# Weight folds and the attention of an expert layer, packed on row groups of TensorE

## The chip, the cores and the metric

The kernel runs on one core of a Trainium2 chip. A core has five engines that run side by side and wait for each other by semaphores: TensorE (PE in the profile; PEld is its weight load), VectorE (DVE), ScalarE (ACT), GpSimd (POOL) and SyncE (SP), which here issues nearly all DMAs. The metric is the device time of one execution in microseconds; the kernel before took 2024.21 us, the median of 3 runs (2023.55 to 2026.4).

## The reference

Sixteen sequences of 64 tokens with 128 features pass through two layers. Each layer has a cross attention to 1601 context rows, a state-space scan, and a feed-forward part. Layer 0's feed-forward part is a mixture of eight experts that begins with a small attention of its own. Two pieces matter here. The cross attention (16 heads of 64):

```python
q = ln @ Wq
kv = kv_input @ Wkv
logits = einsum('bhld,bhsd->bhls', q * scale, k * scale)
out = einsum('bhls,bhsd->bhld', softmax(logits), v)
return out @ Wo
```

and the small attention at the head of the experts (4 heads of 32; keys and values have one head that the four share):

```python
nx = _rmsnorm(X, g1)
Q = (nx @ Wq.T).reshape(B, S, 4, 32).transpose(0, 2, 1, 3)
Kc, Vc = nx @ Wkc.T, nx @ Wvc.T
attn = softmax(einsum('bhsd,btd->bhst', Q, Kc) * scale)
out = einsum('bhst,btd->bhsd', attn, Vc)
X = X + out.transpose(0, 2, 1, 3).reshape(B, S, d) @ Wo.T
```

All numbers are float32.

## The kernel before

**The main loop.** The cross attention is a chain of 64 groups (2 layers, 16 sequences, 2 halves of 8 heads), each with 13 tiles of 128 context rows. `step` does one tile of one group: a scores product `s` of 512 columns (line 651), its copy to `st` by ScalarE and a running maximum `R` by VectorE, and, 21 steps behind, four products `av` of 129 columns (line 713) that average the context with the softmaxed weights. In between lie the maximum's transposes (`tm`), its spread over the partitions (`mb`), the subtraction and the exponential (lines 700 and 701). 832 such steps make the span.

**Folds.** The weights are folded ahead: `fold` multiplies, for each head, the 64 rows of `WqT` with those of `WkT` into `wqk`, and those of `WvT` with `Wo` into `wvo`. Each of the two folds of each of the two layers has 4 groups of 4 heads, so there are 16 groups with 4 products of 128x128 over 64 rows. `raw_pair` (line 317) loads one group's weights with partitions 0 to 63 holding the rows of one head and the four heads side by side in the free dimension. The four results fill one PSUM tile, and one instruction scales and evicts them: ScalarE in two groups of the first fold, VectorE elsewhere.

**The expert layer.** `moe` (line 904) is called for four stages of 256 tokens (`CG` = 2 blocks of 128, `BG` = 4 sequences). After a norm and a transpose to `xT` its small attention goes: queries `mq`, two heads per PSUM tile, each head on partitions 0 to 31 (line 929); keys `mk` on 32 partitions; values `mv`, one sequence after the other on 64 partitions; scores `ms`, 8 products over 32 rows whose 128 outputs are two heads of one sequence; the softmax on VectorE and ScalarE; transposes `mt` to 64 partitions with a copy `pt` each; the averages `ma`, 8 products over 64 rows (line 979); and the output `mo`, for each of the two blocks four accumulated products over 32 rows, one per head (line 988). The router and the experts follow.

**What sets the order.** `run` walks through the steps and puts other work between them: `prep` holds the folds, queries and contexts by their step, and `between` holds the scans, expert layers and feed-forwards, which advance by a budget of estimated VectorE time. Each `yield` with a number charges that budget, and `yield HOP` lets two steps pass. `behind` ties such work behind the instructions of the step before it; apart from that a scheduler orders each engine's instructions when the program is built. Each engine then works through its queue in order, and so does SP's queue of DMA issues.

**PSUM.** Three pools: `pss` with three tiles for scores, `psa` for the averages, and `pst` with three tiles in rotation. `tp` (line 93) hands out the latter to everything else: folds, transposes, expert layers. A fourth request has to wait until the first tile has been evicted.

**Shape of the profile's names.** A float32 product is two records in the trace, with a weight load each; a transpose is one.

Of the kernel before, what the change touches and what calls it, by code (L numbers as in the profile page):

```python
# [32 lines left out]
F32 = mybir.dt.float32  # L33
# [3 lines left out]
AF = mybir.ActivationFunctionType  # L37
ALU = mybir.AluOpType
AX = mybir.AxisListType
# [3 lines left out]
P = 128  # L43
NB, L, D = 16, 64, 128
# [6 lines left out]
H, DH = 16, 64  # L51
# [22 lines left out]
CG = 2  # L74
TG = CG * P
BG = 2 * CG
# [3 lines left out]
class Kernel:  # L80
# [130 lines left out]
    def setup(self):  # L211
# [24 lines left out]

        self.xed = [self.dram.tile([NB, D + 1], F32, tag=f"xed{lay}", name=f"xed{lay}") for lay in range(2)]
        latents, fold, queries, context = self.latents(0, 0), self.fold_qk(0), self.queries(0, 0), self.first_context()
        next(latents)

# [5 lines left out]
        for g in (latents, context, fold, latents, fold, context, queries, queries, context, queries):  # L246
            next(g)
        nc.vector.tensor_scalar_mul(self.nvcol, self.vcol, -1.0)
        self.in_order()
        return (0, context), (1, fold), (5, queries), (8, latents)  # L250

    def setup_rest(self):
# [64 lines left out]
    def raw_pair(self, lay, l, r, g, queue):  # L317


        if lay == 0:  # L320
            t = self.at.tile([P, 2, NQ], F32, tag="st2", name=f"raw{l}{g}", bufs=11)
            pair = [t[:DH, i, :].rearrange("p (h d) -> p h d", h=4) for i in range(2)]
        else:
            pair = [self.at.tile([DH, 4, D], F32, tag="raw", name=f"raw{n}{g}", bufs=3) for n in (l, r)]
        for t, n in zip(pair, (l, r)):
            queue.dma_start(out=t, in_=self.a[f"L{lay}{n}"].rearrange("(h j) d -> j h d", j=DH)[:, g * 4:g * 4 + 4, :])
        return pair

    def fold(self, lay, dst, l, r, scale):

        nc = self.nc
        for g in range(H // 4):
            if (lay, l) == (0, "WqT"):
                raw = self.raw0[g]
            else:
                raw = self.raw_pair(lay, l, r, g, nc.sync)
            if lay == 0 and l == "WvT":
                yield HOP3
            t = self.tp(f"{l}{lay}{g}")
            for k in range(4):  # L340
                nc.tensor.matmul(t[:, k * D:(k + 1) * D], raw[0][:, k, :], raw[1][:, k, :], start=True, stop=True)
            to = dst[:, g * 4:g * 4 + 4, :].rearrange("p h d -> p (h d)")
            if (lay, l) == (0, "WqT") and g < 2:
                nc.scalar.activation(to, t, AF.Copy, scale=scale)
            else:
                nc.vector.tensor_scalar_mul(to, t, scale)
            yield 0.7

    def fold_qk(self, lay):
# [554 lines left out]
    def moe(self, gr):  # L904
        nc, tc, a = self.nc, self.tc, self.a
        X = self.X[:, gr * CG:(gr + 1) * CG, :]
        with tc.tile_pool(name="mo1", bufs=1) as one, tc.tile_pool(name="mo2", bufs=2) as work:
            t1 = lambda shape, name: one.tile(shape, F32, tag=name, name="mo_" + name)
            ld = lambda name, shape, src=None: self.load(name, shape, a[name] if src is None else src, one)
            fWqT, fWkvT = ld("fWqT", [P, D]), ld("fWkvT", [P, 64])  # L910
            fWoT = ld("fWoT", [32, 4, D], a["fWoT"].rearrange("(h k) n -> k h n", k=32))
            WrT = ld("WrT", [P, NE])
            xi, nx, xT = t1([P, CG, D], "xi"), t1([P, CG, D], "nx"), t1([P, TG], "xT")
            mv, (r, rr) = self.moments(X, CG, [LN, LNRMS])
# [6 lines left out]
            self.transpose_tokens(xT, nx, CG, f"mot{gr}", G1)  # L921
            yield HOP

            q, kT, v = t1([32, BG, 4, L], "q"), t1([32, TG], "kT"), t1([L, BG, 32], "v")
            for hh in range(2):
                t = self.tp(f"mq{hh}")
                for k in range(2):
                    h = hh * 2 + k
                    nc.tensor.matmul(t[:32, k * TG:(k + 1) * TG], fWqT[:, h * 32:(h + 1) * 32], xT, start=True, stop=True)
                nc.scalar.copy(  # L930
                    q[:, :, hh * 2:hh * 2 + 2, :],
                    t[:32, :].rearrange("p (h b l) -> p b h l", h=2, l=L),
                )
                yield 0.7
            t = self.tp("mk")
            nc.tensor.matmul(t[:32, :TG], fWkvT[:, :32], xT, start=True, stop=True)
            nc.scalar.copy(kT, t[:32, :TG])
            t = self.tp("mv")
            for b in range(BG):
                nc.tensor.matmul(t[:L, b * 32:(b + 1) * 32], xT[:, b * L:(b + 1) * L], fWkvT[:, 32:], start=True, stop=True)  # L940
            nc.scalar.copy(v.rearrange("p b n -> p (b n)"), t[:L, :BG * 32])
            yield 0.3
            yield HOP

            n = 2 * BG
            shape = [P, n, L]
            sc = t1(shape, "sc")
            t = self.tp("ms")
            for i in range(n):
                b, hp = i // 2, i % 2  # L950
                nc.tensor.matmul(t[:, i * L:(i + 1) * L], q[:, b, 2 * hp:2 * hp + 2, :].rearrange("p h l -> p (h l)"), kT[:, b * L:(b + 1) * L], start=True, stop=True)
            t3 = t.rearrange("p (n l) -> p n l", l=L)
            m = self.sm([P, n], "mm")
            nc.vector.tensor_reduce(m, t3, AX.X, ALU.max)
            nc.vector.tensor_tensor(sc, t3, self.bc(m, shape), ALU.subtract)
            nc.scalar.activation(sc, sc, AF.Exp, scale=32.0 ** -0.5)
            yield 1.4
            yield HOP1
            d, r = self.sm([P, n], "md"), self.sm([P, n], "mr")
            nc.vector.tensor_reduce(d, sc, AX.X, ALU.add)  # L960
# [1 line left out]
            nc.vector.tensor_tensor(sc, sc, self.bc(r, shape), ALU.mult)  # L962
            yield 1.5
            yield HOP
            oT = t1([32, 4, TG], "oT")
            pts = []
            for g in range(n // 4):
                t = self.tp(f"mt{g}")
                for i in range(4):
                    nc.tensor.transpose(t[:L, i * P:(i + 1) * P], sc[:, g * 4 + i, :], self.ident)  # L970
                pt = work.tile([L, 512], F32, tag="pt", name=f"mpt{g}")
                nc.vector.tensor_copy(pt, t[:L, :])
                pts.append(pt)
                yield 0.7
            yield HOP
            for g, pt in enumerate(pts):
                o = self.tp(f"ma{g}")
                for i in range(4):
                    nc.tensor.matmul(o[:32, i * P:(i + 1) * P], v[:, g * 2 + i // 2, :], pt[:, i * P:(i + 1) * P], start=True, stop=True)
                for j in range(2):  # L980
                    b = g * 2 + j
                    nc.scalar.copy(oT[:, :, b * L:(b + 1) * L], o[:32, j * 256:(j + 1) * 256].rearrange("p (h l) -> p h l", h=4))
                yield 0.1
            yield HOP
            o = self.tp("mo")
            for k in range(CG):
                for h in range(4):
                    nc.tensor.matmul(o[:, k * D:(k + 1) * D], oT[:, h, k * P:(k + 1) * P], fWoT[:, h, :], start=(h == 0), stop=(h == 3))
            xs = xi.rearrange("p c d -> p (c d)")
            nc.vector.tensor_tensor(xs, xs, o[:, :CG * D], ALU.add)  # L990
            nc.gpsimd.tensor_tensor(X, X, xi, ALU.add)
# [643 lines left out]
```

## Time and profile before

| | |
|---|---|
| median of 3 runs | 2024.21 us |
| the profiled execution | 2023.47 us |
| its span, first to last instruction | 2021.7 us |
| PE busy | 1974.8 us (98%) |
| VectorE busy | 1563.8 us (77%) |
| ScalarE busy | 1382.3 us (68%) |
| GpSimd busy | 520.5 us (26%) |
| scores `s` (line 651), PE busy | 853.0 us |
| averages `av` (line 713), PE busy | 868.1 us |
| folds (line 341), PE busy, all four | 5.5 + 4.6 + 4.6 + 4.6 us |
| `mq`, `mk`, `mv`, `ms`, `mt`, `ma`, `mo` (four stages) | 7.8, 2.4, 2.6, 8.0, 4.3, 7.7, 8.2 us |

A group's line gives the line of the source, the engine, the operation, what is written from what, the rows and columns of the array that the product uses, the shape, the count, the busy time with the mean length of one record, and the idle time of the engine just before, with what ended it. Products overlap in the array, so a record is longer than the distance to the next one, and busy times of neighbouring groups overlap by that. The rows of ten digits cut the span into 40 slices; a digit is the busy share in tenths.

### The profile page before, as it was taken

The page shows a single profiled execution, that of the slowest core. Times are in us where ns is not written, and L with a number is a line of the kernel's source. Part 1 is how long each engine was busy: PE and PEld are TensorE (multiplying, and loading weights), DVE is VectorE, ACT ScalarE, POOL GpSimd, SP SyncE. Part 2 cuts the span into 40 slices and gives each one's busy share as a digit, 9 for nine tenths or more (in the row PEclk, how much of TensorE's full clock was granted, in tenths as well). Part 3 has the DMA queues.
Part 4 walks back from the last instruction along what each step waited for, and adds up shares of the span by engine and source line. Part 5 has one row for each costly group of instructions (what it writes and reads, how often), then busy time and mean ns, then how long its engine had stood idle before and what let it go on. Part 6 is the DMA issues. An engine that isn't in the chain of part 4 may idle for free. (4 is left out here: it accounts for less than half of the span.)

```text
span 2021.7 us, 32901 instructions
## 1 busy us (share of the span) xinstructions
PE 1974.8 (98%) x12123; PEld 1499.8 (74%) x12123; DVE 1563.8 (77%) x2954; ACT 1382.3 (68%) x2628; POOL 520.5 (26%) x579
## 2 busy tenths in 40 slices
PE   9999999999999989999999999999999999999998
PEld 6777777676777767778777787777778777787787
DVE  6977777886778887676988777898686979778884
ACT  5788878887768887566767657776565656666561
POOL 5111123542123442121543203542111121002000
PEclk9999999999999999999999999999999999999999
DMA  6111112321122321221221102221110110101000
GB/s 175 63 59 46 46 42 84 84 73 50 43 66 84 83 70 36 65 76 45 67 80 51 36 24 72 71 62 51 44 53 18 57 36 22 55 18 36 23 1 22
DMA packets 141805, 110.54 MB, mean 55 GB/s; under 512 B 11458, under 2 KB 127950, under 8 KB 141646
## 3 DMA queue, kind: packets, MB, share of 16 engines
q1 hardware_dynamic: 141102, 108.19, 18.5%
q8 instruction: 96, 1.57, 0.3%
q14 instruction: 63, 0.52, 0.1%
q10 hardware_dynamic: 544, 0.26, 0.0%
HBM read 79.97 MB, written 27.41 MB: 53 GB/s over the span
## 5 line engine op out<-in xcount | busy, mean ns | idle before, releaser
L713 PEld LDWEIGHTS av<-kv,st 128*128 128x128 f32 x6656 | 851.6, 192 | 317.3 <-issue 288.7
L713 PE MATMUL av<-kv,st 128*128 128x129 f32 x6656 | 868.1, 276 | 6.5 <-DVE aq L722 3.9
L651 PE MATMUL s<-qT,kvT 128*128 128x512 f32 x1664 | 853.0, 602 | 17.2 <-DVE R L665 14.2
L700 DVE TENSOR_TENSOR st<-st,mb 128x1024 f32<-128x1024 f32 (+1 forms) x448 | 501.7, 1132 | 1.3 <-PE mb L692 1.1
L701 ACT ACTIVATE st<-st 128x1024 f32<-128x1024 f32 (+1 forms) x448 | 444.9, 997 | 72.1 <-DVE st L700 68.8
L656 ACT ACTIVATE st<-s,mcol 128x512 f32<-128x512 f32 x416 | 283.5, 685 | 221.2 <-PE s L651 178.6
L658 ACT COPY st<-s 128x512 f32<-128x512 f32 x416 | 240.3, 581 | 130.4 <-PE s L651 103.1
L651 PEld LDWEIGHTS s<-qT,kvT 128*128 128x128 f32 x1664 | 259.6, 192 | 84.8 <-DVE R L665 36.1
L663 DVE SCALAR_TENSOR_TENSOR R<-s,mcol,R 128x512 f32<-128x512 f32 x352 | 262.0, 744 | 69.8 <-ACT st L656 68.4
L665 DVE TENSOR_TENSOR R<-s,R 128x512 f32<-128x512 f32 x352 | 240.9, 685 | 90.4 <-ACT st L658 89.3
L762 POOL TENSOR_TENSOR aq<-aq,rd 128x512 f32<-128x512 f32 x63 | 77.6, 1232 | 409.9 <-DVE rd L761 402.6
L565 POOL TENSOR_TENSOR kv<-kv,vec 128x384 f32<-128x384 f32 (+1 forms) x128 | 137.6, 1094 | 151.0 <-PE kt L625 71.7
L866 POOL TENSOR_TENSOR db<-sc_u,bb 128x512 f32<-128x512 f32 x64 | 84.7, 1326 | 134.4 <-DVE h L877 60.8
L883 POOL TENSOR_TENSOR sc_y<-sc_y,h 128x512 f32<-128x512 f32 x60 | 79.9, 1332 | 104.2 <-DVE h L882 80.0
L877 DVE TENSOR_TENSOR_SCAN h<-da,db 128x512 f32<-128x512 f32 x64 | 85.3, 1333 | 0.0
L616 ACT ACTIVATE kv<-kv,coff,crstd 128x128 f32<-128x128 f32 x182 | 76.5, 489 | 5.1 <-POOL coff L613 5.1
L665 DVE TENSOR_TENSOR R<-s,st 128x512 f32<-128x512 f32 x32 | 22.1, 689 | 72.3 <-ACT st L658 72.3
L607 ACT ACTIVATE scr<-kv,cmean 128x128 f32<-128x128 f32 x182 | 72.8, 400 | 6.9 <-DVE cmean L603 3.7
L722 DVE SCALAR_TENSOR_TENSOR aq<-xeb,ee,av 128x129 f32<-128x129 f32 x252 | 72.8, 341 | 1.4 <-PE av L713 1.3
L135 POOL TENSOR_TENSOR crstd<-cvar,neghalf 128x13 f32<-128x13 f32 x14 | 35.0, 2502 | 134.6 <-DVE cvar L611 134.4
L450 PE MATMUL q<-xnT,wqk 128*128 128x128 f32 x512 | 68.8, 277 | 0.0
L450 PEld LDWEIGHTS q<-xnT,wqk 128*128 128x128 f32 x512 | 62.9, 192 | 6.3 <-issue 3.1
(410 smaller groups left out, 1973.5 us busy)
## 6 DMA issues: line engine op xcount, KB each, us to landing
bb<-bcd SPq DMA_DIRECT2D x64, 256.0 KB, 4.4
xh<-kv SPq DMA_DIRECT2D x16, 832.0 KB, 4.8
kv<-xh SPq DMA_DIRECT2D x16, 832.0 KB, 5.5
kvT<-xhT SPq DMA_DIRECT2D x16, 800.0 KB, 4.5
xhT<-kvT SPq DMA_DIRECT2D x15, 800.0 KB, 3.4
kv<-in_ctx_dram SPq DMA_DIRECT2D x15, 768.0 KB, 5.5
ew<-in_e1T_dram SPq DMA_DIRECT2D x36, 64.0 KB, 1.9
ew<-in_e3T_dram SPq DMA_DIRECT2D x36, 64.0 KB, 1.9
```

The lines of the kernel that those rows point to most:

```text
L450: nc.tensor.matmul(t[:, k * P:(k + 1) * P], self.wqk[:, g * 4 + k, :], xnT, start=True, stop=True)
L565: nc.gpsimd.tensor_tensor(kv[:, lo:hi, :D], kv[:, lo:hi, :D], self.row(self.vec[:, w1, :], [P, hi - lo, D]), ALU.mult)
L651: mm = nc.tensor.matmul(s, self.kv_of[lay, b][1][:, i * P:(i + 1) * P], q, start=True, stop=True)
L656: ev = nc.scalar.activation(st, s, AF.Identity, bias=mc)
L658: ev = nc.scalar.copy(st, s)
L663: mx = nc.vector.scalar_tensor_tensor(R, s, mc, last, ALU.add, ALU.max)
L665: mx = nc.vector.tensor_tensor(R, s, last, ALU.max)
L700: nc.vector.tensor_tensor(st, st, self.row(mb, [P, n, NQ]), ALU.subtract)
L701: nc.scalar.activation(st, st, AF.Exp)
L713: nc.tensor.matmul(o, st, self.kv_of[lay, b][0][:, i, :], start=(i == 0 and k % 2 == 0), stop=(i == NT - 1 and k % 2 == 1))
L866: nc.gpsimd.tensor_tensor(db, u, self.row(bb[:, 0, s % 2, :], both), ALU.mult)
L877: nc.vector.tensor_tensor_scan(flat(h), flat(da), flat(db), 0.0, ALU.mult, ALU.add)
```

## The change

The folds, and every product of the small attention that used 32 or 64 of the array's 128 rows, are laid out again.

- `raw_pair` loads the weights as they lie, 128 rows of two heads on 128 partitions, and `fold` multiplies the even heads from partitions 0 to 63 and the odd heads from 64 to 127, in turn, into two PSUM tiles. Each tile is evicted by an instruction of its own.
- The queries of all four heads are one product with 128 outputs, and the keys are made four times over, once under each head, from `fWk4`, a weight that four more DMAs per stage put together.
- The values of odd sequences go to partitions 64 to 127.
- The scores are 16 products over 32 rows with 64 outputs, one for each head and sequence: head `h` works on rows `32h` on, and heads 0 and 1 write the halves of one PSUM tile, 2 and 3 those of another.
- The softmax's maximum and subtraction are done for each of the two tiles.
- The transposed weights of odd sequences go to partitions 64 to 127 of one `pt`.
- The averages are 4 products of 256 columns over 64 rows, alternating between the row halves and two PSUM tiles; eight copies bring the heads to their partitions.
- The output is one product over 128 rows for each block of tokens.

```diff
@@ raw_pair
-            pair = [t[:DH, i, :].rearrange("p (h d) -> p h d", h=4) for i in range(2)]
+            pair = [t[:, i, :2 * D].rearrange("p (m d) -> p m d", m=2) for i in range(2)]
...
-            pair = [self.at.tile([DH, 4, D], F32, tag="raw", name=f"raw{n}{g}", bufs=3) for n in (l, r)]
+            pair = [self.at.tile([P, 2, D], F32, tag="raw", name=f"raw{n}{g}", bufs=3) for n in (l, r)]
...
-            queue.dma_start(out=t, in_=self.a[f"L{lay}{n}"].rearrange("(h j) d -> j h d", j=DH)[:, g * 4:g * 4 + 4, :])
+            queue.dma_start(out=t, in_=self.a[f"L{lay}{n}"].rearrange("(m p) d -> p m d", p=P)[:, 2 * g:2 * g + 2, :])
@@ fold
-            t = self.tp(f"{l}{lay}{g}")
-            for k in range(4):
-                nc.tensor.matmul(t[:, k * D:(k + 1) * D], raw[0][:, k, :], raw[1][:, k, :], start=True, stop=True)
-            to = dst[:, g * 4:g * 4 + 4, :].rearrange("p h d -> p (h d)")
-            if (lay, l) == (0, "WqT") and g < 2:
-                nc.scalar.activation(to, t, AF.Copy, scale=scale)
-            else:
-                nc.vector.tensor_scalar_mul(to, t, scale)
+            ts = [self.tp(f"{l}{lay}{g}{i}") for i in range(2)]
+            for m in range(2):
+                for i in range(2):
+                    half = slice(i * DH, (i + 1) * DH)
+                    nc.tensor.matmul(ts[i][:, m * D:(m + 1) * D], raw[0][half, m, :], raw[1][half, m, :], start=True, stop=True)
+            for i in range(2):
+                to = dst[:, g * 4:g * 4 + 4, :].rearrange("p (m i) d -> p i m d", i=2)[:, i]
+                t = ts[i][:, :2 * D].rearrange("p (m d) -> p m d", m=2)
+                if (lay, l) == (0, "WqT") and g < 2:
+                    nc.scalar.activation(to, t, AF.Copy, scale=scale)
+                else:
+                    nc.vector.tensor_scalar_mul(to, t, scale)
@@ moe
-            fWoT = ld("fWoT", [32, 4, D], a["fWoT"].rearrange("(h k) n -> k h n", k=32))
+            fWoT = ld("fWoT", [P, D])
+            fWk4 = t1([P, 4, 32], "fWk4")
+            for i in range(4):
+                nc.sync.dma_start(out=fWk4[:, i, :], in_=a["fWkvT"][:, :32])
...
-            for hh in range(2):
-                t = self.tp(f"mq{hh}")
-                for k in range(2):
-                    h = hh * 2 + k
-                    nc.tensor.matmul(t[:32, k * TG:(k + 1) * TG], fWqT[:, h * 32:(h + 1) * 32], xT, start=True, stop=True)
-                nc.scalar.copy(
...
-                yield 0.7
+            t = self.tp("mq")
+            nc.tensor.matmul(t[:, :TG], fWqT, xT, start=True, stop=True)
+            nc.scalar.copy(q, t[:, :TG])
+            yield 0.4
             t = self.tp("mk")
-            nc.tensor.matmul(t[:32, :TG], fWkvT[:, :32], xT, start=True, stop=True)
-            nc.scalar.copy(kT, t[:32, :TG])
+            nc.tensor.matmul(t[:, :TG], fWk4.rearrange("p r n -> p (r n)"), xT, start=True, stop=True)
+            nc.scalar.copy(kT, t[:, :TG])
             t = self.tp("mv")
             for b in range(BG):
-                nc.tensor.matmul(t[:L, b * 32:(b + 1) * 32], xT[:, b * L:(b + 1) * L], fWkvT[:, 32:], start=True, stop=True)
-            nc.scalar.copy(v.rearrange("p b n -> p (b n)"), t[:L, :BG * 32])
+                nc.tensor.matmul(t[b % 2 * L:(b % 2 + 1) * L, b // 2 * 32:(b // 2 + 1) * 32], xT[:, b * L:(b + 1) * L], fWkvT[:, 32:], start=True, stop=True)
+            nc.scalar.copy(v.rearrange("p b n -> p (b n)"), t[:, :CG * 32])
...
-            t = self.tp("ms")
-            for i in range(n):
-                b, hp = i // 2, i % 2
-                nc.tensor.matmul(t[:, i * L:(i + 1) * L], q[:, b, 2 * hp:2 * hp + 2, :].rearrange("p h l -> p (h l)"), kT[:, b * L:(b + 1) * L], start=True, stop=True)
-            t3 = t.rearrange("p (n l) -> p n l", l=L)
-            nc.vector.tensor_reduce(m, t3, AX.X, ALU.max)
-            nc.vector.tensor_tensor(sc, t3, self.bc(m, shape), ALU.subtract)
+            ts = [self.tp(f"ms{i}") for i in range(2)]
+            for b in range(BG):
+                for h in range(4):
+                    rows, tok = slice(h * 32, (h + 1) * 32), slice(b * L, (b + 1) * L)
+                    nc.tensor.matmul(ts[h // 2][h % 2 * L:(h % 2 + 1) * L, tok], q[rows, tok], kT[rows, tok], start=True, stop=True)
+            for i in range(2):
+                t3, mi, half = ts[i][:, :TG].rearrange("p (n l) -> p n l", l=L), m[:, i * BG:(i + 1) * BG], [P, BG, L]
+                nc.vector.tensor_reduce(mi, t3, AX.X, ALU.max)
+                nc.vector.tensor_tensor(sc[:, i * BG:(i + 1) * BG, :], t3, self.bc(mi, half), ALU.subtract)
             nc.scalar.activation(sc, sc, AF.Exp, scale=32.0 ** -0.5)
-            yield 1.4
+            yield 1.6
...
+            pt = work.tile([P, 512], F32, tag="pt", name="mpt", bufs=1)
+            for j in range(2):
+                t = self.tp(f"mt{j}")
+                for c in range(CG):
+                    for i in range(2):
+                        nc.tensor.transpose(t[:L, (c * 2 + i) * P:(c * 2 + i + 1) * P], sc[:, i * BG + 2 * c + j, :], self.ident)
+                nc.vector.tensor_copy(pt[j * L:(j + 1) * L], t[:L])
...
+            ts = [self.tp(f"ma{i}") for i in range(2)]
+            for c in range(CG):
+                for i in range(2):
+                    rows = slice(i * L, (i + 1) * L)
+                    nc.tensor.matmul(ts[i][:32, c * 256:(c + 1) * 256], v[rows, c, :], pt[rows, c * 256:(c + 1) * 256], start=True, stop=True)
+            to = oT.rearrange("p (c i l) -> p i c l", i=2, l=L)
+            for i in range(2):
+                o = ts[i][:32, :].rearrange("p (c h l) -> p h c l", c=CG, l=L)
+                for h in range(4):
+                    nc.scalar.copy(to[h * 32:(h + 1) * 32, i], o[:, h])
...
             for k in range(CG):
-                for h in range(4):
-                    nc.tensor.matmul(o[:, k * D:(k + 1) * D], oT[:, h, k * P:(k + 1) * P], fWoT[:, h, :], start=(h == 0), stop=(h == 3))
+                nc.tensor.matmul(o[:, k * D:(k + 1) * D], oT[:, k * P:(k + 1) * P], fWoT, start=True, stop=True)
```

More of the change, by code (lines that the diff above doesn't have):

```diff
@@ L922, in moe @@
             yield HOP
-            q, kT, v = t1([32, BG, 4, L], "q"), t1([32, TG], "kT"), t1([L, BG, 32], "v")
-            for hh in range(2):
-                t = self.tp(f"mq{hh}")
-                for k in range(2):
-                    h = hh * 2 + k
-                    nc.tensor.matmul(t[:32, k * TG:(k + 1) * TG], fWqT[:, h * 32:(h + 1) * 32], xT, start=True, stop=True)
-                nc.scalar.copy(
-                    q[:, :, hh * 2:hh * 2 + 2, :],
-                    t[:32, :].rearrange("p (h b l) -> p b h l", h=2, l=L),
-                )
-                yield 0.7
+            q, kT, v = t1([P, TG], "q"), t1([P, TG], "kT"), t1([P, CG, 32], "v")
+            t = self.tp("mq")
+            nc.tensor.matmul(t[:, :TG], fWqT, xT, start=True, stop=True)
+            nc.scalar.copy(q, t[:, :TG])
+            yield 0.4
             t = self.tp("mk")
-            nc.tensor.matmul(t[:32, :TG], fWkvT[:, :32], xT, start=True, stop=True)
-            nc.scalar.copy(kT, t[:32, :TG])
+            nc.tensor.matmul(t[:, :TG], fWk4.rearrange("p r n -> p (r n)"), xT, start=True, stop=True)
+            nc.scalar.copy(kT, t[:, :TG])
             t = self.tp("mv")
             for b in range(BG):
-                nc.tensor.matmul(t[:L, b * 32:(b + 1) * 32], xT[:, b * L:(b + 1) * L], fWkvT[:, 32:], start=True, stop=True)
-            nc.scalar.copy(v.rearrange("p b n -> p (b n)"), t[:L, :BG * 32])
+                nc.tensor.matmul(t[b % 2 * L:(b % 2 + 1) * L, b // 2 * 32:(b // 2 + 1) * 32], xT[:, b * L:(b + 1) * L], fWkvT[:, 32:], start=True, stop=True)
+            nc.scalar.copy(v.rearrange("p b n -> p (b n)"), t[:, :CG * 32])
             yield 0.3
@@ L964, in moe @@
             yield HOP
[L965 to L973, printed above, removed]
+            oT = t1([P, TG], "oT")
+            pt = work.tile([P, 512], F32, tag="pt", name="mpt", bufs=1)
[5 more added lines that the diff above has]
+                nc.vector.tensor_copy(pt[j * L:(j + 1) * L], t[:L])
                 yield 0.7
             yield HOP
[L976 to L982, printed above, removed]
+            ts = [self.tp(f"ma{i}") for i in range(2)]
[8 more added lines that the diff above has]
+                    nc.scalar.copy(to[h * 32:(h + 1) * 32, i], o[:, h])
                 yield 0.1
```

## The prediction

> **What bounds the kernel now.** I read the page's busy row first, then the slices, then the windows around the changed code.
>
> ```profile
> PE 1974.8 (98%) x12123; PEld 1499.8 (74%) x12123; DVE 1563.8 (77%) x2954; ACT 1382.3 (68%) x2628; POOL 520.5 (26%) x579
> ...
> PE   9999999999999989999999999999999999999998
> DVE  6977777886778887676988777898686979778884
> ```
>
> TensorE (PE) idles 2021.7 - 1974.8 = 46.9 us, and a window query puts 2.7 of it in the first 20 us and 8.9 in the last 57. Elsewhere it is a queue that is nearly never empty; VectorE and ScalarE have a quarter to a third of slack. So a microsecond taken out of the PE stream should come off the end, unless PE then has to wait.
>
> The groups concerned (line, engine, op, tiles, shape, count | busy us, mean ns | idle before):
>
> ```profile
> L988 PE MATMUL mo<-w_fWoT,mo_oT 32*128 32x128 f32 x64 | 8.2, 276 | 0.0
> L951 PE MATMUL ms<-mo_kT,mo_q 32*128 32x64 f32 x64 | 8.0, 273 | 0.0
> L929 PE MATMUL mq<-mo_xT,w_fWqT 128*32 128x256 f32 x32 | 7.8, 383 | 0.0
> L979 PE MATMUL ma<-mpt,mo_v 64*32 64x128 f32 x64 | 7.7, 271 | 0.0
> L1250 PE MATMUL gr<-sd_cT,sd_bT 64*128 64x128 f32 x64 | 6.5, 297 | 1.4 <-DVE gm L1252 1.1 <-ACT sd_cT L1210 0.2
> L341 PE MATMUL WqT<-rawWqT 64*128 64x128 f32 x32 | 4.6, 283 | 0.8 <-DMA rawWqT<-in_L0WkT_dram 0.8
> ```
>
> Each f32 product is two records (64 products `mo`: 4 stages x 8 are x64). The mean is a latency; the cost in the stream is the distance between starts: in the trace's single records 0.112 us for 128 columns (0.109 in `ma`), 0.216 for 256 (`mq`), 0.112 for `ms` (64 columns, a 128-column weight load), 0.058 for `mv` (32 columns, a 64-column load).
>
> The timeline holds the test of the idea. `WvT` is a fold, four products on rows 0 to 63; `gr` is four products too, two on rows 0-63 and two on 64-127, in different PSUM tiles:
>
> ```profile
> 1048.27 1.16 PE L341 MATMUL WvT<-rawWo,rawWvT 64*128 64x128 f32 x8
> 1049.36 1.16 PE L713 MATMUL av<-kv,st 128*128 128x129 f32 x8
> ```
>
> ```profile
> 1540.47 0.72 PE L1250 MATMUL gr<-sd_cT,sd_bT 64*128 64x128 f32 x8
> 1541.12 1.12 PE L651 MATMUL s<-qT,kvT 128*128 128x512 f32 x2
> ```
>
> From its start to the next group's, the fold takes 1.085 us, `gr` 0.652. Its records start in pairs 13 ns apart, pairs 0.112 apart: the halves run side by side. In both, the stream loses 0.19 us at entry and 0.19 at exit.
>
> The clock is the last view:
>
> ```profile
> 826.00:830.00 4.00, 4.00 (x33) 3.65 (x31) 3.79 (x5) 2.65 (x4) 0.00 (x0) 1.00 0.25 74
> 830.00:834.00 4.00, 4.00 (x13) 2.43 (x13) 2.04 (x7) 1.19 (x2) 2.02 (x5) 0.58 0.17 51
> 834.00:838.00 4.00, 4.00 (x12) 2.54 (x11) 1.60 (x5) 0.50 (x1) 0.32 (x2) 0.56 0.21 57
> ```
>
> The seventh entry is the granted clock: from 830.7 to 837.5 it was 0.5. PE was not idle before; it had just run a fold (64 rows) and `mo` (32 rows). That stretch cost 6.8 / 2 = 3.4 us.
>
> **What the Trainium skill says.** "TensorE: Matmul & The Clock Gate", Part 3: small products in different row groups run concurrently, some 4 ns apart, and weight loads overlap a running product only if its row group differs; the trace agrees in kind (13 ns in `gr`; 7 ns between column groups in `se`). "TensorEngine Tiling (Array Packing)", Key Properties: changing the tiling mode drains TensorE; the 0.19 us at each edge agrees. The same page, Gotcha 1: different row tiles cannot access one PSUM bank at once; nothing in the trace shows that, and the new `ms` does it. "TensorE: Matmul & The Clock Gate", Part 1: the clock is half or full, set by recent activity over windows of 3413 ns; the trace has halves of 3.4 and 6.8 us.
>
> **The change, part by part.**
>
> *Folds.* 16 times 4 products. Packed, one costs what `gr` costs: gain 1.085 - 0.652 = 0.433. The changed program's instruction order shows 13 folds whose halves stand adjacent or alternate, and 3 (two of `WvT` in layer 0, one `WqT` in layer 1) with other products between the halves: these change mode twice and lose 0.39. Sum 13 x 0.433 - 3 x 0.39 = 4.5 us. VectorE pays: 14 evictions of 512 columns (0.685) become 28 of 256 (0.415, `mo_xi` and `gm`): +2.0 us, within its slack.
>
> *Queries* (`mq`, per stage): 8 records of 0.216 become 2: 1.30. Full columns also drop the mode change ahead of it; from the last transpose to a working `mq` the trace loses 0.23, of which I take 0.2. Keys stay two records of 256 columns. ScalarE gains: two copies of 0.566 become one of about 0.36.
>
> *Values* (`mv`): the four outputs alternate between column groups. `se` runs two such side by side in one bank, so 8 x 0.058 halves: 0.23.
>
> *Scores* (`ms`): 16 records of 0.112 (1.79) become 32 of 64 columns with a 64-column load, 0.058 each as in `mv`. Four abreast 0.46, two abreast (if a bank takes one row tile at a time) 0.93, one abreast 1.86. I take 0.75: gain 1.04, bounds -0.07 and 1.33. VectorE: 4 passes of 0.415 for 2 of 0.69, +0.28.
>
> *Average* (`ma`): 16 records of 0.109 become 8 of 256 columns on two row groups and two PSUM tiles: 4 x 0.216 in parallel: 1.75 - 0.88 = 0.87 (0 if serial). ScalarE makes 8 copies for 4: about 8 x 0.25 (`mo_v`'s copy) against 4 x 0.357, +0.6; with the query copies about nothing. The transposes `mt` and their two 512-column copies stay as they were.
>
> *Output* (`mo`): 16 records become 4 on 128 rows: 1.34, and both mode changes go, 0.39: 1.73.
>
> Per stage 1.30 + 0.20 + 0.23 + 1.04 + 0.87 + 1.73 = 5.37; four stages 21.5 us.
>
> *Clock.* The work that preceded the half-clock stretch goes from 64 and 32 rows to 128 and shrinks from about 3 us to 1.1: I count its 3.4 us as won (bounds 0 and 3.4; a new stretch of the kind elsewhere would cost 1.7).
>
> *DMAs.* Four more issues per stage on SP's queue (`fWk4`), by the weight loads' rows 0.43 each, 0.47 apart: `WrT`, the expert loads and what follows are 1.9 us later. The copies need about 2.3 us to land; in the tightest stage the loads start at 783.6 and `mq` at 791.3, while the last should land near 788.7, so 2.6 us of cover are left; if it went, `mk` would hold PE. The router needs `WrT` far later. The raw loads keep bytes and row pieces, on 128 partitions for 64: nothing, by the same sizes.
>
> *New wait.* Folds, `ms` and `ma` take two of the three rotating PSUM tiles `tp` at once, in 16 + 4 + 4 = 24 places. The second tile, and the next user, waits for a VectorE or ScalarE eviction of a tile two allocations back instead of three; behind that wait stands the whole in-order PE queue, with the `s` and `av` products, and behind those the softmax on ScalarE and VectorE. By the order, an `s` (0.86) usually stands between. Bounds 0 and 8 us (24 x a third of a microsecond, half an eviction); I take 3.
>
> Sum: 4.5 + 21.5 + 3.4 - 3.0 = 26.4 us. The profiled execution took 2023.5 (span 2021.7 and 1.8 around it) and would take 1997.1; the runs' median 2024.2 is 0.7 above it, so I predict 1998.0 us.
>
> **Rivals.**
>
> *Row groups do not run side by side here* (alternating order, shared banks). Left are queries 6.0, output 6.9, values 0.9, less 1.2 for split folds and 0.3 for `ms`: 12.3, so 2012 us. Against it stands `gr`.
>
> *PE's gain is taken up elsewhere*: VectorE and ScalarE must now do the softmax passes in less time, and PE waits for them. For: VectorE is at 8 tenths in several slices, and PE's few waits are for `R` (17.2 us before `s`). Against: in the window 480 to 560, a whole stage, VectorE is busy 53.1 of 80 us. A third of the 26.4 lost: 1998.0 + 8.8 = 2007 us.
>
> *Slower: the PSUM pair.* PE stands at the 24 pairs until an eviction queued behind a 1.13 us softmax pass (`st`, L700) is through. It cancels the gain of 29.4 from 29.4 / 24 = 1.2 us per pair, and is past 0.2% slower from 1.4; at 1.5 us the time is 2031 us. For: three buffers, VectorE in order. Against: the evicted tile is one product older than the one waited for, and pairs lie several PE microseconds apart.
>
> **How the numbers follow.** Forecast 0.68, softened gain 0.18, no overlap 0.08, slower 0.04, and 0.02 for a balance near zero. 1991 holds all four score streams abreast and no waits (1998.0 - 1.2 - 3.0 = 1993.8) with 3 us for stretches of the clock; 2010 takes in the softened gain and serial scores with full waits (1998.0 + 4.4 + 5.0 = 2007.4). Outside lie the no-overlap and slower cases and little of the forecast. About 0.2%, 4 us, is what a measurement of this kernel can tell from no change: faster 0.94, same 0.02, slower 0.04.
>
> **What would show it.** Fold: about 0.65 us from its start to the next group's, records in pairs. `mo`: 4 records a stage, with no longer first record on either side. `ms`: 32 records in 0.5 to 0.9 us; 1.8 says serial. `ma`: under 0.9 us. No half clock after the layer-1 folds (823 to 839 us before). Wrong if PE's idle time before `WqT`, `WvT`, `ms`, `ma`, `kt` or `mb` grows from near zero to some 10 us with VectorE or ScalarE named, or if `mk` waits for a DMA.

## The result, and the profile after

The changed kernel takes 1994.88 us, the median of 6 runs (1992.59 to 1997.44), beside 2023.88 us for the kernel before in the same runs. The ratio is 0.9872 with a 95% interval of 0.9855 to 0.9889: 25.9 us less (2023.88 x 0.0128). The two medians lie 29.0 us apart, since the six runs of the kernel before are spread over 13 us; this text goes by the ratio. The profiled execution went from 2023.47 to 1997.44 us, its span from 2021.7 to 1995.7. The forecast was 1998.0 us, and 1997.1 for the profiled execution, which turned out to be the slowest of the six; each of its steps can be laid beside the new profile.

The page's busy row and two of its slice rows, kernel after:

```profile
PE 1946.7 (98%) x12083; PEld 1476.7 (74%) x12083; DVE 1562.8 (78%) x2976; ACT 1381.5 (69%) x2642; POOL 519.4 (26%) x579
...
PE   8999999999999999999999999999999999999998
DVE  6977767887878887775998777898787878778784
```

TensorE (PE) lost 28.1 us of busy time and still fills 98% of a shorter span; its idle time grew from 46.9 to 49.0 us. VectorE and ScalarE are as busy as before. So the time came out of the PE stream, as forecast, and a little of it was given back as waiting.

The groups of the changed products, kernel after:

```profile
L995 PE MATMUL mo<-w_fWoT,mo_oT 128*128 128x128 f32 x16 | 2.4, 275 | 0.0
L956 PE MATMUL ms<-mo_kT,mo_q 32*64 32x64 f32 x128 | 2.8, 223 | 0.0
L934 PE MATMUL mq<-mo_xT,w_fWqT 128*128 128x256 f32 x8 | 2.4, 380 | 0.0
L985 PE MATMUL ma<-mpt,mo_v 64*32 64x256 f32 x32 | 4.2, 382 | 0.0
L942 PE MATMUL mv<-w_fWkvT,mo_xT 128*64 128x32 f32 x32 | 1.7, 228 | 1.0 <-ACT mo_q L935 1.0
L344 PE MATMUL WqT<-rawWkT,rawWqT 64*128 64x128 f32 x32 | 3.6, 295 | 2.4 <-DMA rawWkT<-in_L1WkT_dram 1.1 <-ACT mo_oT L990 0.8 <-DVE R L670 0.5
```

The mean of a record hardly moved (`mo` 276 to 275 ns); the counts and the distances between starts did. `ms` has twice the records (128 for 64) and a third of the busy time (2.8 for 8.0 us), because four records now start within 0.02 us of each other.

Two folds and their neighbours in the timeline, kernel after (start, length, instruction, idle before):

```profile
821.28 0.72 PE L344 MATMUL WqT<-rawWkT,rawWqT 64*128 64x128 f32 x8
821.93 1.98 PE L656 MATMUL s<-qT,kvT 128*128 128x512 f32 x4
...
826.75 0.72 PE L344 MATMUL WqT<-rawWkT,rawWqT 64*128 64x128 f32 x8 [1.05 <-DMA rawWkT<-in_L1WkT_dram]
827.40 1.16 PE L718 MATMUL av<-kv,st 128*128 128x129 f32 x8
```

A packed fold hands over after 0.65 us, to the hundredth what `gr` showed before; the fold of before took 1.085.

To compare the two streams I charge each PE record with the time from the end of the record before it to its own end; over all records that adds up to the stream (the time PE takes, its waits included), 2018.8 us before and 1992.4 after. By groups, in us:

| group | before | after | saved |
|---|---|---|---|
| output `mo` | 7.91 | 1.78 | 6.12 |
| queries `mq` | 7.49 | 1.73 | 5.76 |
| scores `ms` | 7.70 | 2.50 | 5.20 |
| average `ma` | 7.45 | 3.94 | 3.51 |
| values `mv` | 2.33 | 2.54 | -0.22 |
| folds, all 16 | 20.08 | 15.80 | 4.28 |
| `s` of the main loop | 756.16 | 751.74 | 4.42 |
| `tm` of the main loop | 28.87 | 31.27 | -2.40 |
| all else | | | -0.3 |
| stream | 2018.8 | 1992.4 | 26.4 |

The rows of `s` and `tm` are waits and clock rather than work. `s` waits less for `R` (14.2 us before, 11.1 after), and the half-clock stretch at 830 us, which lay on `s` and `av`, is gone. `tm` has a new wait of 2.1 us. Two other rows hold waits as well: 1.0 us in `mv` after, and in the folds 1.6 before and 2.5 after, which there cancels against half clock: the fold at 831.7 us took 2.0 us before, where others took 1.09.

### The profile page after: what moved, and what is told of

It is laid out like the page before. It is cut to its first block, busy times and chain, and to the rows that moved or that the text cites. A ratio compares the mean times of both kernels' runs of the same rounds, so it can differ in the third digit from the quotient of the medians.

```text
span 1995.7 us, 32852 instructions
## 1 busy us (share of the span) xinstructions
PE 1946.7 (98%) x12083; PEld 1476.7 (74%) x12083; DVE 1562.8 (78%) x2976; ACT 1381.5 (69%) x2642; POOL 519.4 (26%) x579
## 5 line engine op out<-in xcount | busy, mean ns | idle before, releaser
L656 PE MATMUL s<-qT,kvT 128*128 128x512 f32 x1664 | 851.0, 601 | 14.7 <-DVE R L670 11.1
```

The source lines that it names most:

```text
L656: mm = nc.tensor.matmul(s, self.kv_of[lay, b][1][:, i * P:(i + 1) * P], q, start=True, stop=True)
```

## The experiments

My theory: the stream shrinks because row groups work side by side and full-row products need fewer passes; the two parts add up; the clock follows the rows in use; the price is a few waits on the shared PSUM tiles. The rivals said that the overlap is not there, that a part of the gain is softened away, or that the PSUM pairs eat it. All ratios are to the kernel before, run beside the experiment on the same chip.

### Each part alone

e1 is the kernel before with the packed folds only, that is the part of the change's diff that lies in `raw_pair` and `fold`:

```diff
@@ fold
-            t = self.tp(f"{l}{lay}{g}")
...
+            ts = [self.tp(f"{l}{lay}{g}{i}") for i in range(2)]
...
+                    nc.tensor.matmul(ts[i][:, m * D:(m + 1) * D], raw[0][half, m, :], raw[1][half, m, :], start=True, stop=True)
```

e2 is the kernel before with the part in `moe` only:

```diff
@@ moe
-            fWoT = ld("fWoT", [32, 4, D], a["fWoT"].rearrange("(h k) n -> k h n", k=32))
+            fWoT = ld("fWoT", [P, D])
+            fWk4 = t1([P, 4, 32], "fWk4")
...
```

> The kernel before with the packed folds alone. If the gain is what the PE stream saves, 13 folds save 0.43 us each and 3 split ones lose 0.39: 4.5 us under the kernel before, less the 2.1 us wait of the transposes `tm` for an eviction of `wvo` that the profile after shows, so some 2.4 us. If the pair of PSUM tiles makes more trouble than that, no gain or a loss.

> The kernel before with the expert layer's part alone. If the parts add up by the PE stream: 21.5 us under the kernel before (queries 1.5, values 0.2, scores 1.25, averages 0.87, output 1.73 a stage). If the clock made a good part of the difference, the half-clock stretch beside the layer-1 folds is still there or not, and the time moves by up to 3.4 us with it. If folds and expert layer help each other, clearly less than 21.

e1: 0.9974 (0.9963 to 0.9986), 5.3 us less, twice the 2.4 expected. e2: 0.9891 (0.9875 to 0.9908), 22.0 us less, for 21.5. The clock is in both. For every run beside the experiments the mean granted clock is known: 0.9965 of full speed over the 26 runs of the kernel before, 0.9977 over the 7 of e1 and 0.9978 over the 4 of e2, and 0.0012 of 2020 us is 2.4 us. That is about what e1 gained beyond its expectation. The product of both ratios is 0.9865, within the interval of the whole change, so the parts add to within some 4 us. The rival of 2007 us is shut out by the whole change itself: the upper end of its interval is 2001.4 us (2023.88 x 0.9889). In their traces the groups gained what they gain together (in e2 `mo` 5.93, `mq` 5.76, `ms` 5.20, `ma` 3.51).

### Two PSUM tiles without packing

An edit of the kernel before:

```diff
@@ fold
-            t = self.tp(f"{l}{lay}{g}")
-            for k in range(4):
-                nc.tensor.matmul(t[:, k * D:(k + 1) * D], raw[0][:, k, :], raw[1][:, k, :], start=True, stop=True)
+            ts = [self.tp(f"{l}{lay}{g}{i}") for i in range(2)]
+            for m in range(2):
+                for i in range(2):
+                    nc.tensor.matmul(ts[i][:, m * D:(m + 1) * D], raw[0][:, 2 * m + i, :], raw[1][:, 2 * m + i, :], start=True, stop=True)
...
```

The raw weights stay on 64 partitions, so all products share the rows 0 to 63; only the pair of tiles and the two evictions are new.

> The kernel before with each fold's four products written to two PSUM tiles and evicted in two instructions, but all on rows 0 to 63: the pair without the packing. Stream alone: 3 split folds at 0.39, 1.2 us above the kernel before. If the pair makes PE wait: 3 to 4 us above, with the wait of `tm` for `wvo` in it. If the pair were the danger that the slower rival held it for, over 10 us above.

1.0002 (0.9994 to 1.001), 0.4 us more. The pair costs too little to see, 2 us at most. This ends the rival of 2031 us for the folds, which needed 1.4 us a pair; the pairs of `ms` and `ma` no run takes apart. It also sizes the overlap: between e3 and e1 only the layout of the weights on one row half or two differs, and that is 5.7 us (2020 x 0.0028), give or take 3. In the traces the folds take 18.3 us of the stream in e3 and 13.3 in e1.

### The output on 32 rows again

An edit of the kernel after, as are all that follow:

```diff
@@ moe
-            fWoT = ld("fWoT", [P, D])
+            fWoT = ld("fWoT", [32, 4, D], a["fWoT"].rearrange("(h k) n -> k h n", k=32))
...
-                    nc.scalar.copy(to[h * 32:(h + 1) * 32, i], o[:, h])
+                    nc.scalar.copy(to[:, h, i], o[:, h])
...
-                nc.tensor.matmul(o[:, k * D:(k + 1) * D], oT[:, k * P:(k + 1) * P], fWoT, start=True, stop=True)
+                for h in range(4):
+                    nc.tensor.matmul(o[:, k * D:(k + 1) * D], oT[:, h, k * P:(k + 1) * P], fWoT[:, h, :], start=(h == 0), stop=(h == 3))
```

> The kernel after with the output product laid out as before: four accumulated products over 32 rows for each block. Stream: 4 x 1.73 = 6.9 us above the kernel after, that is some 19 us under the kernel before. If the products over 32 rows also bring the clock down, 1.7 to 3.4 us more and a half-clock stretch next to a fold and `mo`.

0.9912 (0.9897 to 0.9926), against 0.9872 for the whole change: the one product over 128 rows is worth about 8 us (2020 x 0.0040). `mo` went from 1.78 to 7.91 us in the stream, which is 6.1, and the profiled executions differ by 5.9 (2003.36 - 1997.44); what the ratio has beyond that is within its interval, and the clock over all runs gives as much: 0.9967 on the mean here (4 runs), 0.9977 after (6), some 2 us. In the two profiled executions the clock moved, but its sum did not: both have 13.7 us at half clock, this one with a stretch of 3.4 us at 825.0 and others gone. The timeline of this kernel just before that stretch:

```profile
821.63 2.05 PE L996 MATMUL mo<-w_fWoT,mo_oT 32*128 32x128 f32 x16
823.61 0.71 PE L344 MATMUL WqT<-rawWkT,rawWqT 64*128 64x128 f32 x4
824.25 0.49 PE L718 MATMUL av<-kv,st 128*128 128x129 f32 x2
824.66 0.93 PE L344 MATMUL WqT<-rawWkT,rawWqT 64*128 64x128 f32 x4
```

PE is not idle here. In the kernel before, too, products over 32 and 64 rows stand directly ahead of the clock's fall at 830.7 us:

```profile
827.09 1.15 PE L341 MATMUL WqT<-rawWkT,rawWqT 64*128 64x128 f32 x8
828.17 2.05 PE L988 MATMUL mo<-w_fWoT,mo_oT 32*128 32x128 f32 x16
830.15 1.59 PE L651 MATMUL s<-qT,kvT 128*128 128x512 f32 x2
```

In e1 (folds packed, output on 32 rows) and in e2 (the reverse) there is no half clock around 825 us. But there is none in e3 either, which packs nothing: there an `s` lies between that fold and `mo`. So low rows can bring the clock down, and whether they do hangs on what falls close together, as the section on the clock shows.

### The scores one head after the other

```diff
@@ moe
-            for b in range(BG):
-                for h in range(4):
+            for h in range(4):
+                for b in range(BG):
```

> The kernel after with the score products issued head by head, four sequences of one row group in a row, instead of head after head for each sequence. If the row groups overlap whatever the order (as `gr` did, two products of one row group and then two of the other), the 32 records of `ms` take 0.5 us a stage as in the kernel after. If PE starts products strictly in order, one row group runs at a time: 32 x 0.058 = 1.9 us a stage, 5.3 us in all.

One stage's `ms` in the timeline, this kernel:

```profile
492.75 1.54 PE L956 MATMUL ms<-mo_kT,mo_q 32*64 32x64 f32 x32
494.22 1.12 PE L656 MATMUL s<-qT,kvT 128*128 128x512 f32 x2
```

and the kernel after:

```profile
495.67 0.69 PE L956 MATMUL ms<-mo_kT,mo_q 32*64 32x64 f32 x32
496.30 1.12 PE L656 MATMUL s<-qT,kvT 128*128 128x512 f32 x2
```

Neither number of the expectation came out: `ms` takes 5.87 us of the stream for 2.50, 0.84 more per stage, where full overlap would give nothing and none at all 1.4. The single records say why. Within a head they start 0.058 us apart. The first record of the next head starts 6 ns after the fifth of the eight before it: heads begin at 492.754, 493.043, 493.330 and 493.618, every 0.288 us instead of 8 x 0.058 = 0.46. So only neighbouring heads overlap, by their last and first three records; why no further is not shown. In the alternating order four records start 7 ns apart and the next four 0.058 later. The time, 0.9887 (0.9861 to 0.9912), agrees with 3.4 us more than after, but cannot tell them from nothing.

### Extra products on 32 rows and on 128

Twenty products more after each output, whose result nobody reads: extra work, the same in number and columns, over 32 rows in one kernel (e6, shown) and over 128 in the other (e7, with `[:128]` for `[:32]`).

```diff
@@ moe
+            pad = self.tp("pad")
+            for _ in range(20):
+                nc.tensor.matmul(pad[:, :P], self.ident[:32], self.ident[:32], start=True, stop=True)
```

> The kernel after with 20 more products (identity by identity, results unused) over 32 rows behind each stage's output product. Stream: 40 records x 0.112 = 4.5 us and two mode changes of 0.2 a stage, 19.5 us above the kernel after. If the clock follows the rows in use and not the time in use: a half-clock stretch at each stage's padding, 1.7 us or more for each, 26 us and more above the kernel after.

> The same 20 products over all 128 rows: 4.5 us a stage, 17.9 us above the kernel after, and no half-clock stretch at the padding under either theory.

With 32 rows: 1.0016 (1.0004 to 1.0029); with 128: 0.9967 (0.9957 to 0.9977). Above the change's own 0.9872 that is 29 and 19 us, for 26 and more and 17.9 expected. Nearly all of the 10 us between the two is the clock: it was 0.9922 on the mean over the 15 runs with 32 rows and 0.9967 over the 18 with 128, and 0.0045 of 2020 us is 9.1. The timeline of one block and the windows behind it (PE, PEld, DVE, ACT and POOL busy, granted PE clock, DMA share, GB/s), 32 rows:

```profile
510.31 6.05 PE L998 MATMUL pad<-ident 32*128 32x128 f32 x40
```

```profile
510.00:514.00 4.00, 4.00 (x34) 3.88 (x33) 4.00 (x10) 1.94 (x2) 1.77 (x2) 0.93 0.06 12
514.00:518.00 4.00, 4.00 (x14) 2.90 (x13) 0.42 (x2) 0.63 (x1) 1.31 (x4) 0.50 0.00 0
518.00:522.00 4.00, 4.00 (x22) 3.12 (x21) 2.11 (x5) 1.09 (x2) 0.00 (x0) 0.71 0.00 0
```

and 128 rows:

```profile
513.70 4.63 PE L998 MATMUL pad<-ident 128*128 128x128 f32 x40
```

```profile
514.00:518.00 4.00, 4.00 (x38) 4.00 (x38) 3.90 (x9) 1.58 (x3) 1.67 (x3) 1.00 0.00 0
518.00:522.00 4.00, 4.00 (x27) 2.90 (x27) 2.02 (x5) 1.64 (x3) 1.28 (x4) 1.00 0.00 0
```

PE is busy without a gap in both. With 32 rows the clock falls to half at each of the four blocks, for 3.4 or 6.8 us; with 128 rows at none. So the clock's activity is not only time in use: the rows in use count. "TensorE: Matmul & The Clock Gate", Part 1, of the Trainium skill says that the clock follows activity over free-running windows of 3413 ns; the lengths 3.4 and 6.8 us agree, but the page says nothing of rows, and these two runs show them.

### Where the new waits come from

The waits view of the kernel after has some lines that the kernel before had not. The three looked at here are:

```profile
PE tm L679 <- DVE wvo L351: 2.1, 1, 2.1
...
PE WqT L344 <- DMA rawWkT<-in_L1WkT_dram: 1.1, 1, 1.1
PE mv L942 <- ACT mo_q L935: 1.0, 1, 1.0
```

I first read the `tm` wait as the price of the three folds whose halves are split by other products. e8 gives those three the old layout, one tile and 64 rows, within the kernel after:

```diff
@@ raw_pair, fold
+    def packed(lay, l, g):
+        return not ((lay, l) == (0, "WvT") and g >= 2 or (lay, l, g) == (1, "WqT", 0))
...
+            if not self.packed(lay, l, g):
+                t = self.tp(f"{l}{lay}{g}")
+                for k in range(4):
+                    nc.tensor.matmul(t[:, k * D:(k + 1) * D], raw[0][:, k, :], raw[1][:, k, :], start=True, stop=True)
...
```

> The kernel after with the three folds that the instruction order splits (groups 2 and 3 of `WvT` in layer 0, group 0 of `WqT` in layer 1) laid out as before in one PSUM tile. Stream: 3 x 0.39 = 1.2 us less, and the 2.1 us wait of `tm` goes: some 3 us under the kernel after, 0.15%. If the split folds and the pair cost nothing, the same time as the kernel after.

0.9882 (0.9862 to 0.9902): no difference from the whole change that can be measured, where 3 us less was expected. The three folds are in one piece again, but the wait is still there, unchanged, since it belongs to an earlier, unsplit fold (timeline of e8):

```profile
40.06 0.66 PE L697 MATMUL tm<-ident,R 128*128 128x128 f32 x4 [2.11 <-DVE wvo L369]
```

So two more kernels went at that wait itself. e9 takes the second tile of a fold from the pool of the scores; e10 lets ScalarE evict it.

```diff
@@ fold, e9
-            ts = [self.tp(f"{l}{lay}{g}{i}") for i in range(2)]
+            ts = [self.tp(f"{l}{lay}{g}0"), self.pss.tile([P, NQ], F32, tag="s", name=f"{l}{lay}{g}1")]
@@ fold, e10
-                if (lay, l) == (0, "WqT") and g < 2:
+                if i == 1 or (lay, l) == (0, "WqT") and g < 2:
```

> The kernel after, with the second tile of each fold taken from the three score tiles (pool pss) instead of the three rotating tiles. If the 2.1 us wait of tm for the eviction wvo comes from two fold tiles being held in the same rotation, it goes, and with it the half clock that follows it near 40 us (1.7 us): some 2 to 4 us under the kernel after. If the wait comes from VectorE being late there anyway, it stays or shows up as a wait of s for a score tile, and the time is that of the kernel after or above it, since a score tile is then missing for the pipeline of s.

> The kernel after, with the eviction of the odd heads' fold tile moved from VectorE to ScalarE, so that the two evictions of a fold need not queue on one engine. If the wait of tm for wvo is for the second of two evictions in VectorE's queue, it shrinks from 2.1 to under 1 us and the time falls by 1 to 3 us. If ScalarE is no sooner (it copies st there), the wait remains and names ScalarE: no difference from the kernel after within 2 us.

The wait for `wvo` went in both, and the time did not: 0.9898 (0.988 to 0.9916) and 0.9898 (0.9881 to 0.9916), if anything above the change's 0.9872. e9 is not a clean test: with a score tile taken away, PE's waits before the folds grew from 2.5 to 5.9 us. The PE lines with a wait around the same place show what came instead, in e9:

```profile
35.41 0.71 PE L344 MATMUL WvT<-rawWvT 64*128 64x128 f32 x8 [1.20 <-DMA rawWvT<-in_L0Wo_dram]
...
40.40 0.66 PE L679 MATMUL tm<-ident,R 128*128 128x128 f32 x4 [1.28 <-DVE R L670]
```

and in e10:

```profile
36.43 1.38 PE L399 MATMUL ge<-xeT,wkq0s 128*128 128x16 f32 x8 [2.40 <-ACT wkq0s L396]
```

From 30 to 42 us PE stands idle for 2.1 us after, 2.5 in e9 and 2.4 in e10 (1.0 before). The timeline of the kernel after, all engines, shows the chain behind it:

```profile
33.71 2.46 POOL L135 TENSOR_TENSOR crstd<-crstd,neghalf 128x13 f32<-128x13 f32 x1 [1.50 <-DVE crstd L592]
...
37.22 0.28 POOL L595 TENSOR_SCALAR coff<-coff 128x13 f32<-128x13 f32 x1
...
37.53 0.88 ACT L600 ACTIVATE kv<-kv,coff,crstd 128x128 f32<-128x128 f32 x2 [2.67 <-POOL coff L595]
38.31 0.56 ACT L663 COPY st<-s 128x512 f32<-128x512 f32 x1
...
38.91 0.69 DVE L670 TENSOR_TENSOR R<-s,R 128x512 f32<-128x512 f32 x1 [3.32 <-ACT st L663]
39.52 0.74 DVE L351 TENSOR_SCALAR wvo<-WvT 128x256 f32<-128x256 f32 x2
...
39.99 0.75 PE L679 MATMUL tm<-ident,R 128*128 128x128 f32 x4 [2.11 <-DVE wvo L351]
```

Read from the bottom: `tm` wants the tile that `wvo` empties; `wvo` stands behind `R` in VectorE's queue; `R` waits for the copy `st`; `st` stands behind the normalisation of the context in ScalarE's queue; and that waits for GpSimd's `coff`, which is done at 37.5 us. VectorE was idle for 3.3 us before `R`. The last line names the eviction, but what is late is GpSimd's `coff`, behind its own `crstd` of 2.46 us, which in turn had waited for VectorE. The eviction can't have been worth much: `tm` also reads that `R`, which ended at 39.60 us, so without `wvo` it would have started 0.4 us earlier at most. In the kernel before ScalarE waited for the same `coff` (done at 36.8 us), and PE, slower there, filled more of that time with products. A PE that is ahead gets no further than this chain lets it, which fits that taking away the tile, or the eviction, moved the wait and gained no time. (In e10 the copy `wkq0s` that PE waits for stands in the same ScalarE queue, behind the first `kv` that waited for `coff`.) That a faster normalisation there would gain the 2 us was not tried.

The other two are small. The fourth `rawWkT` of layer 1 was covered before, and in e1, where the expert layer is the old one; in e2, which has the new expert layer, the wait is 0.9 us. After, its load is issued at 822.16 us behind two context loads on SP's queue, and the fold now comes before it has landed. And `mv` reads nothing of `q`, so it can wait for the copy `mo_q` only because it takes the PSUM tile that `mq` had.

### The clock after a wait of PE

All half-clock stretches of the kernel before but the one at 830 us, and all of the kernel after, begin within 2.3 us after PE has waited for one thing for 1.8 us or more; the end of the span, where PE has run out of work, left aside. In all twelve profiled executions (the first 15 us left out), by the length of the wait, and counting a half clock that begins in the wait or within 3.5 us of its end:

| PE idle for | waits | half clock follows |
|---|---|---|
| 1.4 to 1.6 us | 14 | 0 |
| 1.6 to 1.8 us | 19 | 4 |
| 1.8 to 2.2 us | 26 | 10 |
| over 2.2 us | 16 | 14 |

The same wait of 2.11 us at 38 us was followed by half clock after, in e1, e4 and e8, but not in e6 and e7. The traces say why. In each of the twelve executions all changes of the clock from 10 us on lie whole multiples of 3.4133 us apart, to 2 ns, and the first of them at another offset each time: the clock is decided in windows that run freely. After, in e1, e4 and e8 the wait lies within one window; in e6 and e7 a boundary, at 39.0 and 39.1 us, splits it. And one sum per window covers waits and low rows together: PE's busy time in it, each record charged as in the table of the streams and weighted by the share of the 128 rows in use (row groups that run side by side taken together). All windows at full clock between 10 and 1960 us, by that sum:

| busy time by rows, of 3.41 us | windows | half clock in the next |
|---|---|---|
| under 1.45 us | 26 | 26 |
| 1.45 to 1.75 us | 26 | 8 |
| 1.75 to 2.0 us | 28 | 1 |
| over 2.0 us | 6732 | 0 |

The window ahead of 830.7 us in the kernel before has no idle time, but by rows only 1.44 us; the one with the same products in e3 has 2.0. Weighting by columns too sorts the windows about as well, so whether columns count stays open. The one case between 1.75 and 2.0 us is e9's stretch at 61 us, behind a microsecond of transposes over 16 rows and a split fold.

Each stretch of 3.4 us costs 1.7 us. Much of the spread between runs of one kernel comes from this: of the 36 runs of the kernel before beside e5 to e8, the seven with a mean clock of 0.998 took 2014.8 to 2018.5 us, and the ten with 0.995 took 2023.0 to 2025.6.

## Why the prediction was right, step by step

**Queries, output, average, folds.** Right in mechanism and size: 6.0, 6.9, 3.5 and 4.5 us forecast, 5.76, 6.12, 3.51 and 4.28 in the groups' own records. The output was forecast with the mode change after it (0.8 us in all), which the accounting charges to the next group; ahead of the queries 0.14 us a stage was saved, for 0.2. The folds' number holds the cancelling waits and half clock named above. The three split folds were forecast to lose; in the trace each takes some 1.3 us for the 1.09 of before, but e8, good to 4 us, cannot tell the 1.2 us forecast from nothing.

**Scores.** The gain was undersized: 1.04 us a stage forecast, from 0.75 us for the 32 records between "four abreast 0.46" and "two abreast 0.93". The records span 0.477 us: four abreast, and 1.30 a stage was gained. The doubt came from the skill's "TensorEngine Tiling (Array Packing)", Gotcha 1, by which row tiles cannot access one PSUM bank at once. Here heads 0 and 1 write one PSUM tile on different partitions, and start 7 ns apart. The measurement decides: this sharing did not serialise them.

**Values.** 0.9 us forecast, 0.2 lost. The step that failed is the list of new waits: I counted the pairs and overlooked that a single tile, `mv`'s, can come back to one still being copied (1.0 us). Without that wait 0.8 of the 0.9 us is there.

**Clock.** 3.4 us forecast, 1.7 found in the profiled pair: half clock fell from 17.1 to 13.7 us. Over all runs whose clock is known the mean is 0.9964 for the kernel before (73 runs) and 0.9977 after (6), some 2.5 us. The stretch at 830 us went, and the reason given holds as far as low rows count: in e4 and e6 they bring such stretches back, full rows in e7 do not. That they do so only where a window holds enough of them was not foreseen; e3 lost the stretch with the old rows. A new one appeared at 40.4 us behind the new wait, the "new stretch of the kind elsewhere" that I had priced at 1.7 and left out of the likeliest sum.

**New waits.** 3.0 us forecast for the PSUM pairs. Found: 2.1 us at `tm`, named for a pair's eviction but set by the chain from GpSimd; 0.8 of `WqT` for the copies `mo_oT`; 1.1 for a DMA; 1.0 at `mv`. Against these stand 3.1 us less of `s` waiting for `R` and the loads that PE waited for before; in all PE's idle time grew by 2.1 us. The size was about right, the cause was not: e3 and e10 show that the folds' pairs as such cost nothing that can be measured. The 0.8 us behind `mo_oT` may be a price of the pair `ma`; no run shows it. The load of `rawWkT`, costed at nothing because its bytes stay, was late by 1.1 us: what hid it was the time that PE took before it, and that was removed.

**VectorE.** +2.0 us for the fold evictions forecast, +1.3 found (6.2 + 4.7 for 5.5 + 4.1), hidden as said.

So the sum's 1997.1 for the profiled execution met 1997.4 because its errors nearly cancel, which is luck: scores 1.0 us better, values 1.1 and clock 1.7 worse, and waits of other kinds than expected with 3.1 us less for `R` on the other side. The parts that the new layout takes out of the stream, 24.7 us found for 26.0 forecast, are no luck.

## What to carry to other kernels

On a PE that is 98% busy, small products are worth laying out for the rows they use: 28 us of busy time went while the other engines stayed as busy as they were, and the saving could be added up from distances between starts that the old trace already held. Alternate the row groups product by product, for long runs in one group overlap only at their edges. When PE becomes faster, look along the whole chain behind its next wait before adding buffers: the wait named VectorE's eviction, and what was late lay several links further, on GpSimd.

## What the runs showed of the hardware

- Products over 32 rows of four row groups ran four abreast, 32 records in 0.477 us, though two heads each write one PSUM tile, on different halves of its partitions.
- In head-by-head order the same 32 records took 1.32 us from first to last start, and only the last and first three records of neighbouring heads overlapped.
- Forty records over 32 rows brought half clock in 4 of 4 places, forty over 128 rows in 0 of 4, PE being busy without a gap in both.
- In twelve executions every change of the clock after 10 us lay on a grid of 3.4133 us. Between 10 and 1960 us, a full-clock window with less than 1.45 us of row-weighted busy time was followed by half clock in 26 of 26 cases, one with more than 2.0 us in 0 of 6732.
- A wait of PE of over 2.2 us was followed by half clock in 14 of 16 cases, one of 1.4 to 1.6 us in 0 of 14.
